# Two heads per penalty product, the penalty's bound on ScalarE, and other PSUM banks in the 16-head attention of the last layer

## The chip, the cores and the metric

The kernel runs on one core of a Trainium2 chip. A core has five engines that work side by side[...]: PE (TensorE, matrix products into the accumulator memory PSUM), VectorE (DVE in the profile), ScalarE (ACT), GpSimd (POOL) and SyncE (SP, which here issues most of the DMA transfers). Each engine takes its instructions in the order of the program. The metric is the device time of one execution in microseconds (us).

## The reference, cut to what matters

The network has four layers on an input of 16 x 256 x 128 numbers. Each layer normalizes, computes an attention and a feed-forward branch from the same normalized input, and adds their gated product to the residual. The change concerns the attention of the last layer, with 16 heads of width 8:

```python
g = sigmoid(hidden_states @ Wg + bg)                 # one number per token
Z_I, Z_J = g, swapaxes(g, 1, 2)
res = (1 - Z_I) * maximum(1 - Z_I - Z_J, 0) + Z_I * minimum(1 - Z_I + Z_J, 1)
scope = clip(power(s - 2, 1 - g) + 2 - abs_ij, 1e-32, 1)
log_pen = log(maximum(res * scope, 1e-32))           # 256 x 256 per batch element
scores = q @ k.T / sqrt(8) + log_pen                 # the same for all 16 heads
ctx = softmax(scores) @ v
```

The kernel does not add the logarithm. It multiplies the exponentials of the plain scores by the penalty itself, which is bounded from below by 1e-32.

## The kernel before, in words

**Where it stands.** `attn8` is called twice: by the first layer without a penalty, and by `attn3` for the last layer with one. The second call is the last stage of the kernel; after it only the last output remains to be stored. All earlier work of the last layer (its feed-forward branch in `xn`, the gates in `gates3`) is complete by then.

**Tiles.** There are 256 heads in all (16 batch elements, called batches here, of 16 heads). One head's scores are 256 x 256, held as 128 partitions x 512 numbers, which is one PSUM bank. Queries and keys are laid out so that a head occupies 8 of a group of 32 partitions, with a ninth row for the maximum.

**The loop.** The loop over `n` (line 446) works on two heads in each step. `scores(n, m)` (line 313) issues four matrix products that alternate: the first scores `pa` of head `n` (L322), queries by keys, and the second scores `pb` of head `m = n - 14` (L332), keys by queries, in which the maximum found from the first scores takes part. VectorE reduces `pa` to the negated row maximum `nmax` (L343). ScalarE takes the exponential of `pb` into `e` (L348). The tile `pb` then is free, and `e` waits for its product with the penalty.

**The product with the penalty.** `weaken(m)` (L311) multiplies `e` in place by the penalty tile `pens[m // 16]` of its batch. It is issued one step after the exponential, on VectorE for heads 2, 5, 9, 12 and 15 of each batch and on GpSimd for the other eleven.

**Around the heads.** Every eighth step (u is the step within eight, k within sixteen) other pieces are issued: at u = 1 `shifted` (L359, L365) transposes the maxima of the last eight heads and adds them to the queries, and `values` makes the value tile; at u = 3 `turn` (L400 to L408) transposes and divides the result of eight heads; at u = 5 `weigh` (L374) multiplies eight heads' `e` by the values, and ScalarE copies the result (L385). `project` (L272 to L288) makes queries and keys for two batches, sends them through memory and reads them back on SP's queue. `done` (line 1589) multiplies a finished batch by the feed-forward branch (L1594), adds it to the residual (L1595), and two steps later stores it from SP (L1592).

**The penalty.** `penalty(b)` in `attn3` (line 1511) returns a list of small functions that together make the penalty of a batch. The loop takes them one by one (line 479): ScalarE makes the four parts (L1532 to L1541), GpSimd the distance term `near` (L1544), two products `inner` (L1547, L1548) and their sum `summed` (L1551), and VectorE at k = 15 the product with the scope (L1554) and the lower bound (L1555). They are one batch ahead: batch b + 1's penalty is finished at step 15 of batch b and first used some 16 steps later.

**Buffers.** The first scores have three PSUM banks (`psa`), the second scores three (`psb`), all other products two (`psm`). There are 22 tiles `e`. A product into `pa` waits for the reduction three heads before, a product into `pb` for the exponential three heads before.

**What sets the order.** `pin(mark)` (line 484) chains each engine's instructions in the order in which the program issued them, so no planner reorders this stage: an instruction that waits holds back everything behind it on its engine.

Of the kernel before, what the change touches and what calls it, by code (L numbers as in the profile page):

```python
# [10 lines left out]
F32 = mybir.dt.float32  # L11
# [8 lines left out]
P = 128  # L20
B = 16
S = 256
# [51 lines left out]
class Net:  # L74
# [137 lines left out]
    def attn8(self, w, bias=None, wout=None, penalty=None, done=None):  # L212
# [16 lines left out]
        with ExitStack() as ctx:  # L229
            cp = ctx.enter_context(tc.tile_pool(name="at_c", bufs=1))  # L230
            pool = ctx.enter_context(tc.tile_pool(name="at", bufs=2))
            small = ctx.enter_context(tc.tile_pool(name="at_s", bufs=2))
            ep = ctx.enter_context(tc.tile_pool(name="at_e", bufs=22))
            dram = ctx.enter_context(tc.tile_pool(name="at_d", bufs=2, space=DRAM))
            psa = ctx.enter_context(tc.tile_pool(name="at_pa", bufs=3, space=PSUM))
            psb = ctx.enter_context(tc.tile_pool(name="at_pb", bufs=3, space=PSUM))
            psm = ctx.enter_context(tc.tile_pool(name="at_pm", bufs=2, space=PSUM))

            wqk = [self.load(cp, w[n], "w" + n) for n in "qk"]
# [64 lines left out]
                            va[:, q, :, 0:8], src, vadd.rearrange("p (h e) -> p h e", e=8)  # L304
                        )

            qas, es, pens, pos, zs = {}, {}, {}, {}, {}

            def weaken(m):
                eng = nc.vector if m % 16 in (2, 5, 9, 12, 15) else nc.gpsimd  # L310
                eng.tensor_mul(es[m], es[m], pens[m // 16])  # L311

            def scores(n, m):

                pa = psa.tile([P, 2, S], F32, name="pa") if n is not None else None
                pb = psb.tile([P, 2, S], F32, name="pb") if m is not None else None
                for t in range(2):
                    ts = slice(t * P, (t + 1) * P)
                    if n is not None:
                        b, h = divmod(n, 16)  # L320
                        r, g = 32 * (h % 4), h // 4
                        nc.tensor.matmul(  # L322
                            pa[:, t, :],
                            qbuf[b % 4][r : r + 32, g, ts],
                            kbuf[b % 4][r : r + 32, g, :],
                            start=True,
                            stop=True,
                        )
                    if m is not None:
                        b, h = divmod(m, 16)  # L330
                        r, g = 32 * (h % 4), h // 4
                        nc.tensor.matmul(  # L332
                            pb[:, t, :],
                            kbuf[b % 4][r : r + 32, g, ts],
                            qas[m // 8][r : r + 32, g % 2, :],
                            start=True,
                            stop=True,
                        )
                if penalty is not None and m is not None and m > 0:
                    weaken(m - 1)  # L340
                if n is not None:
                    u = n % 8
                    nc.vector.tensor_reduce(  # L343
                        nbuf[n // 8 % 2][:, :, u // 4, u % 4, 8], pa, AX.X, ALU.max, negate=True
                    )
                if m is not None:
                    e = ep.tile([P, 2, S], F32, name="e")
                    nc.scalar.activation(e, pb, AF.Exp, scale=scale)  # L348
                    es[m] = e
                    if penalty is not None and m == H - 1:  # L350
                        weaken(m)

            def shifted(i):

# [91 lines left out]
            for n in range(H + 4 * 8):  # L446
# [27 lines left out]
                if penalty is not None:  # L474
                    k = n % 16
                    if k == 0 and b + 2 < B:
                        parts[b + 2] = penalty(b + 2)
                        parts[b + 2].pop(0)()
                    if k in (3, 4, 5, 6, 7, 8, 9, 11, 13) and b + 1 < B:
                        parts[b + 1].pop(0)()  # L480
                    elif k == 15 and b + 1 < B:
                        pens[b + 1] = parts.pop(b + 1).pop(0)()
# [1016 lines left out]
    def attn3(self, g, dr, done):  # L1499
# [3 lines left out]
        with ExitStack() as ctx:  # L1503
# [2 lines left out]
            pool2 = ctx.enter_context(tc.tile_pool(name="a3_2", bufs=2))  # L1506
            pool3 = ctx.enter_context(tc.tile_pool(name="a3_3", bufs=3))
            dist = self.const("dist", cp, view="p (k q) -> p k q", k=2)
            wide = lambda t: t.rearrange("p (o q) -> p o q", o=1).to_broadcast([P, 2, S])

            def penalty(b):
# [31 lines left out]
                def near():  # L1543
                    nc.gpsimd.tensor_sub(sc, wide(pw), dist)  # L1544

                def inner():
                    nc.gpsimd.tensor_mul(lo, lo, wide(u))  # L1547
                    nc.gpsimd.tensor_mul(hi, hi, wide(gi))  # L1548

                def summed():  # L1550
                    nc.gpsimd.tensor_add(lo, lo, hi)  # L1551

                def bounded():
                    nc.vector.scalar_tensor_tensor(pen, sc, 1.0, lo, ALU.min, ALU.mult)  # L1554
                    nc.vector.tensor_scalar_max(pen, pen, 1e-32)  # L1555
                    return pen

                return [fetch, rest, low(0), low(1), high(0), high(1), rather, near, inner, summed, bounded]

            self.attn8(  # L1560
                {n: a["L3_attn_W" + n] for n in "qkv"},
# [6 lines left out]
    def layer3(self, out):  # L1568
# [5 lines left out]
        with ExitStack() as ctx:  # L1574
# [14 lines left out]
            def done(b, store):  # L1589
                ts = slice(2 * b, 2 * b + 2)  # L1590
                if store:
                    nc.sync.dma_start(out[:, ts, :], self.x[:, ts, :])  # L1592
                else:
                    nc.vector.tensor_mul(self.s[:, ts, :], self.s[:, ts, :], X[:, ts, :])  # L1594
                    nc.vector.tensor_add(self.x[:, ts, :], self.x[:, ts, :], self.s[:, ts, :])  # L1595

            self.attn3(g, dr, done)

# [375 lines left out]
```

## Time and profile before

| | |
|---|---|
| median of 3 runs | 3046.34 us (3040.31 to 3046.86) |
| profiled execution | 3046.38 us |
| its span, first to last instruction | 3044.6 us |
| mean TensorE clock granted | 0.879 |
| busy, share of the span: PE, VectorE, ScalarE, GpSimd | 83%, 69%, 49%, 44% |
| first product of the last stage (L322) | about 2612 us |
| last product of first scores (L322) | 3019.9 us |
| VectorE, ScalarE, GpSimd busy in 2820 to 2846 us | 22.92, 12.77, 20.86 us of 26 |

The profile is one execution. A row of groups gives line, engine, operation, written and read tiles with shapes and a count, then the busy time, the mean duration, the idle time of the engine just before, and what ended that idle time. Where two engines exclude each other, the time that an instruction stands inside the exclusion is part of its duration, so a long duration may be a wait. The clock column is the share of full speed that TensorE was granted. PE counts as busy from start to end of overlapping products, so a busy PE can still be slow.

### The profile page before, as it was taken

Reading aid. Unit: us, or ns where it says so; the run is one execution under the profiler, and the core shown is the slowest. Engines: PE = TensorE matmul, PEld = TensorE weight load, DVE = VectorE, ACT = ScalarE, POOL = GpSimd, SP = SyncE. Lnnn points to the kernel's source line nnn. Section 1 sums busy time; section 2 is a strip of 40 time slices with the busy share of each in tenths; the row PEclk is TensorE's granted clock in tenths of the full one; section 3 lists DMA queues with packets and bytes.
Section 4 is the critical chain, followed back from the end, with each engine's and each line's share of the span. In section 5 each row is a group of like instructions: output and inputs, shape, how many; then the busy total and the mean of one; then the engine's idle time right before and its main releaser. Section 6 shows DMA issues by size and latency. Waiting matters only on the chain.

```text
span 3044.6 us, 49166 instructions
## 1 busy us (share of the span) xinstructions
PE 2516.5 (83%) x17715; PEld 1627.3 (53%) x17743; DVE 2088.2 (69%) x4302; ACT 1506.0 (49%) x3339; POOL 1348.7 (44%) x1247
## 2 busy tenths in 40 slices
PE   5999882679665799999834899988799989798998
PEld 3666571556431466666513466665466655555555
DVE  4666433335487789888874778844687855588887
ACT  1555461223333566666531577751477764454554
POOL 2000002123227566656665455531455552487777
PEclk8999995879876899999965899998899999788888
DMA  2111002000113566666521000000100000211110
GB/s 64 29 29 29 6 3 99 1 16 15 40 57 123 153 178 184 182 175 185 170 72 49 15 13 15 13 5 1 44 14 14 15 10 1 49 37 38 31 39 10
DMA packets 155196, 168.95 MB, mean 55 GB/s; under 512 B 22817, under 2 KB 102874, under 8 KB 154954
## 3 DMA queue, kind: packets, MB, share of 16 engines
q1 hardware_dynamic: 146378, 147.71, 17.7%
q0 software_dynamic: 6496, 17.05, 1.7%
q8 instruction: 141, 2.31, 0.3%
q10 hardware_dynamic: 2080, 1.05, 0.1%
q14 instruction: 101, 0.83, 0.1%
HBM read 127.57 MB, written 29.79 MB: 52 GB/s over the span
## 4 chain that ended last, share of the span: by engine, by line
PE 29%; DVE 27%; ACT 7%; POOL 3%; issue 3%; DMA 2%; SPq 1%; another core or an unknown queue 0%; DVEq 0%; ACTq 0%; POOLq 0%
PE py L1145 4%; ACT p L1787 3%; PE pa L322 3%; DVE st L1124 2%; DVE nmax L343 2%; DVE rot L1713 2%; DVE ss L1712 2%; DVE sn L1716 2%; PE ph L1365 2%; PE py L1391 2%; DVE nm L1778 2%; PE ps L1768 2%; PE ph L1908 2%; PE pa L1000 1%; PE ph L1912 1%
## 5 line engine op out<-in xcount | busy, mean ns | idle before, releaser
L322 PE MATMUL pa<-kT,qT 32*128 32x256 f32 x2048 | 420.3, 443 | 54.6 <-DVE nmax L343 35.6
L343 DVE TENSOR_REDUCE nmax<-pa 128x2 f32<-128x512 f32 x512 | 332.1, 684 | 149.0 <-PE pb L332 123.4
L348 ACT ACTIVATE e<-pb 128x512 f32<-128x512 f32 x512 | 286.0, 595 | 295.4 <-PE pb L332 293.2
L332 PE MATMUL pb<-qa,kT 32*128 32x256 f32 x2048 | 414.6, 429 | 0.9 <-ACT e L348 0.9
L322 PEld LDWEIGHTS pa<-kT,qT 32*128 32x128 f32 x2048 | 273.9, 206 | 171.5 <-DVE nmax L343 80.8
L1135 POOL TENSOR_TENSOR hc<-st,cn 128x512 f32<-128x512 f32 x207 | 264.3, 1278 | 207.9 <-DVE dbb L1121 85.8
L1145 PE MATMUL py<-hc,ident 128*128 128x512 f32 x512 | 296.1, 670 | 68.6 <-DVE hc L1135 41.8
L1124 DVE TENSOR_TENSOR_SCAN st<-dab,dbb 128x512 f32<-128x512 f32 x256 | 312.5, 1221 | 33.0 <-ACT dab L1114 3.4
L311 POOL TENSOR_TENSOR e<-e,pen 128x512 f32<-128x512 f32 x176 | 241.7, 1390 | 102.4 <-ACT e L348 102.1
L332 PEld LDWEIGHTS pb<-qa,kT 32*128 32x128 f32 x2048 | 268.0, 199 | 7.9 <-ACT e L348 2.6
L1114 ACT ACTIVATE dab<-dl,A_log 128x512 f32<-128x512 f32 x256 | 181.5, 719 | 147.4 <-DVE st L1124 107.8
L1787 ACT ACTIVATE p<-ps,nm,rl 128x128 f32<-128x128 f32 x512 | 227.8, 466 | 30.0 <-DVE nm L1780 29.2
L1796 POOL TENSOR_TENSOR p<-p,den 128x512 f32<-128x512 f32 x128 | 133.0, 1040 | 231.5 <-DVE den L1795 225.9
L158 POOL TENSOR_SCALAR ln_r<-ln_mv 128x4 f32<-128x4 f32 x32 | 7.4, 232 | 493.5 <-DVE ln_st L168 419.4
L1698 PE MATMUL pm<-wqkv,hT 128*128 128x512 f32 x384 | 208.8, 658 | 17.9 <-DVE hT L1692 8.0
L1721 POOL TENSOR_TENSOR rot<-rot,sn 128x512 f32<-128x512 f32 x128 | 162.5, 1270 | 108.7 <-DVE sn L1716 71.3
L1121 DVE TENSOR_TENSOR dbb<-du,bn 128x512 f32<-128x512 f32 x256 | 203.1, 793 | 6.0
L1145 PEld LDWEIGHTS py<-hc,ident 128*128 128x128 f32 x512 | 94.6, 208 | 170.7 <-DVE hc L1135 68.3
L1711 ACT ACTIVATE sq<-pm 128x512 f32<-128x512 f32 x128 | 75.0, 617 | 136.2 <-PE pm L1698 136.2
L1768 PE MATMUL ps<-kT,qT 64*64 64x128 f32 x2048 | 137.2, 290 | 0.0
L374 PE MATMUL pm<-e,vaug 128*32 128x256 f32 x2048 | 133.2, 403 | 0.0
L1768 PEld LDWEIGHTS ps<-kT,qT 64*64 64x64 f32 x2048 | 91.2, 138 | 72.9 <-issue 70.1
(372 smaller groups left out, 5638.4 us busy)
## 6 DMA issues: line engine op xcount, KB each, us to landing
bn<-dr SPq DMA_DIRECT2D x128, 256.0 KB
cn<-dr SPq DMA_DIRECT2D x128, 256.0 KB
w<-in_L_ffn_W_dram SPq DMA_DIRECT2D x94, 256.0 KB
qkd<-qk SPq DMA_DIRECT2D x32, 256.0 KB
v<-v SPq DMA_DIRECT2D x64, 128.0 KB
f_y<-y SPq DMA_DIRECT2D x47, 128.0 KB
f_x<-zero POOLq DMA_DIRECT2D x8, 704.0 KB
xr<-f_x SPq DMA_DIRECT2D x44, 128.0 KB
```

The lines of the kernel that those rows point to most:

```text
L311: eng.tensor_mul(es[m], es[m], pens[m // 16])
L322: nc.tensor.matmul(pa[:, t, :], qbuf[b % 4][r : r + 32, g, ts], kbuf[b % 4][r : r + 32, g, :], start=True, stop=True,)
L332: nc.tensor.matmul(pb[:, t, :], kbuf[b % 4][r : r + 32, g, ts], qas[m // 8][r : r + 32, g % 2, :], start=True, stop=True,)
L343: nc.vector.tensor_reduce(nbuf[n // 8 % 2][:, :, u // 4, u % 4, 8], pa, AX.X, ALU.max, negate=True)
L348: nc.scalar.activation(e, pb, AF.Exp, scale=scale)
L1121: mul = nc.vector.tensor_mul(db, d["du"][:, h, :], d["bn", n])
L1124: nc.vector.tensor_tensor_scan(d["st", r], d.pop(("da", r)), db, 0.0, ALU.mult, ALU.add)
L1135: ins = eng.tensor_mul(d["hc", r], d.pop(("st", r)), d["cn", r // 2])
L1145: nc.tensor.matmul(d["py", h], self.ident, d.pop(("hc", r)), start=(n == 0), stop=(n == N - 1))
L1698: nc.tensor.matmul(pj, hTs[b % 3][:, t * P : (t + 1) * P], d["qkv"][:, j * 512 : (j + 1) * 512], start=True, stop=True,)
L1768: nc.tensor.matmul(ps[i][64 * half : 64 * half + 64, c, w, :], qT[f, 2 * u + c, q0 : q0 + 64], kT[f, 2 * u + c, keys[half] : keys[half] + ...
L1787: nc.scalar.activation(p[:, c, w, :], ps[i][:, c, w, :], AF.Exp, scale=r[:, w, 0, h + 2 * c : h + 2 * c + 1], bias=nm[:, c, w : w + 1], ac ...
```

## The change

With a penalty, `attn8` has four banks for first scores and two for second ones, and 11 tiles `e` of twice the size in place of 22. Two neighbouring heads share one such tile; `weaken` is issued in every second step for a pair, with the penalty tile read twice through a repeating dimension, on VectorE for the pairs that begin at heads 2 and 8 of a batch and on GpSimd for the other six. The lower bound of the penalty leaves VectorE: ScalarE computes Relu(pen - 1e-32) + 1e-32 in two activations, `over` and `least_of`. The penalty's parts are taken at other steps: `near` at k = 8, the two products of `inner` at 9 and 10, `summed` at 11, the VectorE product `bounded` at 13, `over` at 14 and `least_of` at 15. In `done` the last sum goes from VectorE to GpSimd. The call without a penalty keeps its banks and tiles.

```diff
--- before.py
+++ after.py
@@ -230,10 +230,10 @@
             cp = ctx.enter_context(tc.tile_pool(name="at_c", bufs=1))
             pool = ctx.enter_context(tc.tile_pool(name="at", bufs=2))
             small = ctx.enter_context(tc.tile_pool(name="at_s", bufs=2))
-            ep = ctx.enter_context(tc.tile_pool(name="at_e", bufs=22))
+            ep = ctx.enter_context(tc.tile_pool(name="at_e", bufs=11 if penalty else 22))
             dram = ctx.enter_context(tc.tile_pool(name="at_d", bufs=2, space=DRAM))
-            psa = ctx.enter_context(tc.tile_pool(name="at_pa", bufs=3, space=PSUM))
-            psb = ctx.enter_context(tc.tile_pool(name="at_pb", bufs=3, space=PSUM))
+            psa = ctx.enter_context(tc.tile_pool(name="at_pa", bufs=4 if penalty else 3, space=PSUM))
+            psb = ctx.enter_context(tc.tile_pool(name="at_pb", bufs=2 if penalty else 3, space=PSUM))
             psm = ctx.enter_context(tc.tile_pool(name="at_pm", bufs=2, space=PSUM))
 
             wqk = [self.load(cp, w[n], "w" + n) for n in "qk"]
@@ -304,11 +304,14 @@
                             va[:, q, :, 0:8], src, vadd.rearrange("p (h e) -> p h e", e=8)
                         )
 
-            qas, es, pens, pos, zs = {}, {}, {}, {}, {}
+            qas, es, pairs, pens, pos, zs = {}, {}, {}, {}, {}, {}
 
             def weaken(m):
-                eng = nc.vector if m % 16 in (2, 5, 9, 12, 15) else nc.gpsimd
-                eng.tensor_mul(es[m], es[m], pens[m // 16])
+
+                eng = nc.vector if m % 16 in (2, 8) else nc.gpsimd
+                pen = pens[m // 16].rearrange("p (o k) q -> p o k q", o=1)
+                eng.tensor_mul(pairs[m], pairs[m], pen.to_broadcast([P, 2, 2, S]))
+                del pairs[m]
 
             def scores(n, m):
 
@@ -336,19 +339,24 @@
                             start=True,
                             stop=True,
                         )
-                if penalty is not None and m is not None and m > 0:
-                    weaken(m - 1)
+                if penalty is not None and m is not None and m > 0 and m % 2 == 0:
+                    weaken(m - 2)
                 if n is not None:
                     u = n % 8
                     nc.vector.tensor_reduce(
                         nbuf[n // 8 % 2][:, :, u // 4, u % 4, 8], pa, AX.X, ALU.max, negate=True
                     )
                 if m is not None:
-                    e = ep.tile([P, 2, S], F32, name="e")
+                    if penalty is None:
+                        e = ep.tile([P, 2, S], F32, name="e")
+                    else:
+                        if m % 2 == 0:
+                            pairs[m] = ep.tile([P, 2, 2, S], F32, name="e")
+                        e = pairs[m - m % 2][:, m % 2]
                     nc.scalar.activation(e, pb, AF.Exp, scale=scale)
                     es[m] = e
                     if penalty is not None and m == H - 1:
-                        weaken(m)
+                        weaken(m - 1)
 
             def shifted(i):
 
@@ -476,7 +484,7 @@
                     if k == 0 and b + 2 < B:
                         parts[b + 2] = penalty(b + 2)
                         parts[b + 2].pop(0)()
-                    if k in (3, 4, 5, 6, 7, 8, 9, 11, 13) and b + 1 < B:
+                    if k in (2, 3, 4, 5, 6, 7, 8, 9, 10, 11, 13, 14) and b + 1 < B:
                         parts[b + 1].pop(0)()
                     elif k == 15 and b + 1 < B:
                         pens[b + 1] = parts.pop(b + 1).pop(0)()
@@ -1506,6 +1514,9 @@
             pool2 = ctx.enter_context(tc.tile_pool(name="a3_2", bufs=2))
             pool3 = ctx.enter_context(tc.tile_pool(name="a3_3", bufs=3))
             dist = self.const("dist", cp, view="p (k q) -> p k q", k=2)
+            least = cp.tile([P, 2], F32, name="least")
+            nc.gpsimd.memset(least[:, 0:1], -1e-32)
+            nc.gpsimd.memset(least[:, 1:2], 1e-32)
             wide = lambda t: t.rearrange("p (o q) -> p o q", o=1).to_broadcast([P, 2, S])
 
             def penalty(b):
@@ -1543,19 +1554,27 @@
                 def near():
                     nc.gpsimd.tensor_sub(sc, wide(pw), dist)
 
-                def inner():
-                    nc.gpsimd.tensor_mul(lo, lo, wide(u))
-                    nc.gpsimd.tensor_mul(hi, hi, wide(gi))
+                def inner(t, by):
+                    return lambda: nc.gpsimd.tensor_mul(t, t, wide(by))
 
                 def summed():
                     nc.gpsimd.tensor_add(lo, lo, hi)
 
                 def bounded():
                     nc.vector.scalar_tensor_tensor(pen, sc, 1.0, lo, ALU.min, ALU.mult)
-                    nc.vector.tensor_scalar_max(pen, pen, 1e-32)
+
+
+                def over():
+                    nc.scalar.activation(pen, pen, AF.Relu, bias=least[:, 0:1])
+
+                def least_of():
+                    nc.scalar.activation(pen, pen, AF.Identity, bias=least[:, 1:2])
                     return pen
 
-                return [fetch, rest, low(0), low(1), high(0), high(1), rather, near, inner, summed, bounded]
+                return [
+                    fetch, rest, low(0), low(1), high(0), high(1), rather, near,
+                    inner(lo, u), inner(hi, gi), summed, bounded, over, least_of,
+                ]
 
             self.attn8(
                 {n: a["L3_attn_W" + n] for n in "qkv"},
@@ -1592,7 +1611,7 @@
                     nc.sync.dma_start(out[:, ts, :], self.x[:, ts, :])
                 else:
                     nc.vector.tensor_mul(self.s[:, ts, :], self.s[:, ts, :], X[:, ts, :])
-                    nc.vector.tensor_add(self.x[:, ts, :], self.x[:, ts, :], self.s[:, ts, :])
+                    nc.gpsimd.tensor_add(self.x[:, ts, :], self.x[:, ts, :], self.s[:, ts, :])
 
             self.attn3(g, dr, done)
```

## The prediction

> **What bounds the kernel now.** The diff reaches only the last stage, the second call of `attn8`. I read its stage windows first, then its groups, the order of time on VectorE, and one-microsecond windows around a stall. The first windows set one stretch of the first layer's call of `attn8` (no penalty) beside one of the last layer's. Columns: stretch, then busy us and instructions of PE, weight load, VectorE, ScalarE, GpSimd; the clock granted to TensorE; DMA.
>
> ```profile
> 226.00:252.00 26.00, 25.10 (x306) 16.68 (x302) 18.79 (x38) 13.64 (x26) 0.00 (x0) 1.00 0.05 14
> 2820.00:2846.00 26.00, 24.31 (x212) 14.68 (x204) 22.92 (x34) 12.77 (x24) 20.86 (x15) 0.83 0.16 36
> ```
>
> The same products go at 306 matmul records per 26 us there and at 212 here. The starts of L1554 give the pace: 2654.21 to 2997.91 us is 13 batches, 26.44 us each. In thirteen 26-us windows (2638 to 2976) the means are VectorE 22.46 busy, GpSimd 20.67, ScalarE 12.94, PE 213 records at clock 0.848. At the first call's 305 records per 26 us, PE needs 26.44 x 213/305 = 18.5 us per batch at full clock. The lost clock adds 0.152 x 26.44 = 4.0 us, and 3.9 us is left for stalls.
>
> Groups of the steady part (2630 to 3000 us); after the shapes: busy us, mean ns, idle before:
>
> ```profile
> L322 PE MATMUL pa<-kT,qT 32*128 32x256 f32 x905 | 214.1, 453 | 34.4 <-DVE nmax L343 34.1
> L311 POOL TENSOR_TENSOR e<-e,pen 128x512 f32<-128x512 f32 x156 | 213.6, 1386 | 94.3 <-ACT e L348 94.1
> L343 DVE TENSOR_REDUCE nmax<-pa 128x2 f32<-128x512 f32 x226 | 148.0, 681 | 42.5 <-PE pb L332 42.5
> L322 PEld LDWEIGHTS pa<-kT,qT 32*128 32x128 f32 x904 | 137.3, 212 | 101.0 <-DVE nmax L343 61.8 <-issue 20.4 <-DVE s L408 5.4
> L311 DVE TENSOR_TENSOR e<-e,pen 128x512 f32<-128x512 f32 x70 | 76.8, 1097 | 3.9 <-ACT e L348 3.9
> L1554 DVE SCALAR_TENSOR_TENSOR pen<-sc,lo 128x512 f32<-128x512 f32 x15 | 25.7, 1711 | 2.4 <-POOL lo L1551 2.4
> L1555 DVE TENSOR_SCALAR pen<-pen 128x512 f32<-128x512 f32 x15 | 20.6, 1374 | 0.5
> L1595 DVE TENSOR_TENSOR x<-x,s 128x256 f32<-128x256 f32 x13 | 17.8, 1373 | 0.4
> L1594 DVE TENSOR_TENSOR s<-s,xn 128x256 f32<-128x256 f32 x13 | 13.7, 1051 | 0.0
> ```
>
> PE's stalls end on VectorE's reduction of the first scores, L343. And VectorE's other instructions are long: the shortest of the same forms took 0.68 (L311), 0.69 (L1554) and 0.43 us (L1555, L1595). The excess per batch is 5 x 0.42 + 1.02 + 0.94 + 0.94 + 0.62 = 5.6 us. In order of time:
>
> ```profile
> 2886.82 1.05 DVE L1594 TENSOR_TENSOR s<-s,xn 128x256 f32<-128x256 f32 x1
> 2887.91 1.38 DVE L1595 TENSOR_TENSOR x<-x,s 128x256 f32<-128x256 f32 x1
> 2889.20 0.68 DVE L343 TENSOR_REDUCE nmax<-pa 128x2 f32<-128x512 f32 x1
> 2889.81 1.15 DVE L311 TENSOR_TENSOR e<-e,pen 128x512 f32<-128x512 f32 x1
> 2892.11 1.74 DVE L1554 SCALAR_TENSOR_TENSOR pen<-sc,lo 128x512 f32<-128x512 f32 x1
> 2893.89 1.37 DVE L1555 TENSOR_SCALAR pen<-pen 128x512 f32<-128x512 f32 x1
> ```
>
> From step 12 to 17 of a batch only one reduction passes in some 2 us, PE's three first-score banks run full, and its clock falls:
>
> ```profile
> 2894.00:2895.00 1.00, 0.40 (x4) 0.00 (x0) 1.00 (x1) 0.47 (x1) 1.00 (x2) 1.00 0.32 99
> 2895.00:2896.00 1.00, 0.09 (x2) 0.09 (x2) 1.00 (x3) 0.13 (x1) 1.00 (x1) 1.00 0.48 82
> 2897.00:2898.00 1.00, 1.00 (x6) 0.69 (x4) 1.00 (x2) 0.60 (x1) 1.00 (x1) 0.50 0.57 95
> ```
>
> PE idles 1.5 us in two, and then runs at half clock. This comes back in every batch, for 3 to 11 us.
>
> **What the Trainium skill says.** "SBUF — State Buffer", section "Who interferes with whom": a VectorE instruction with two SBUF inputs and a GpSimd instruction that reads SBUF exclude each other for the whole instruction. The trace agrees: 0.69 us for L1554 alone, 1.74 beside GpSimd. "TensorE: Matmul & The Clock Gate", section "HAM oscillation — how this bites in real kernels": idle PE halves its clock. The trace agrees on the half, but less idleness than the page's 3.4 us is enough here (1.5 us above). Its opening table: ScalarE, VectorE and GpSimd queues are strict FIFO, so one waiting instruction holds what follows.
>
> **The change, part by part** (per batch; "held" is a duration less the 0.04 to 0.09 us in which the next one overlaps it).
>
> 1. Products for two heads. No 128x1024 product with a penalty is in the trace, but GpSimd's 128x1024 L1070 took 2.35 us and VectorE's L1062 1.23; a repeated operand costs GpSimd nothing (L1548, 1.27). GpSimd: 11 x 1.23 = 13.5 becomes 6 x 2.31 = 13.9. VectorE, without waits: 5 x 0.60 = 3.0 becomes 2 x 1.14 = 2.3. The unknown, a slower repeated pattern, I bound from 0 to 10% (1.6 us) and take 0.
> 2. Bound: VectorE loses L1555, 0.36 of work and 0.94 of waiting. ScalarE gains two 128x512 activations, 0.52 held by L1541, so 12.9 becomes 14.0 of 26: hidden by its idle time (uncovered, 15 x 1.04 = 16 us), unless it waits. It can: `over` (step 14) stands behind `bounded` (step 13), and later exponentials stand behind it.
> 3. The sum L1595 goes to GpSimd: VectorE loses 0.36 and 0.94 of waiting; GpSimd gains 0.69 (its 128x256 L592 took 0.73). The output store on SP waits for it some 2 us longer; behind it in SP's queue stand the next project's transfers, not used for 13 steps. Nothing on the path (uncovered, 2 us in every second batch, 16 us).
> 4. Steps spread out: the same instructions; GpSimd still has difference, two products, sum and one pair ahead of `bounded`.
> 5. Banks 4 + 2: PE may lead the reductions by four heads, the exponentials by two.
>
> VectorE's work falls from 22.46 - 5.6 = 16.8 to 15.4 us. Contended instructions fall from nine to four (two pairs, L1594, L1554), but each may meet a GpSimd instruction of 2.31 instead of 1.23. I bound the four waits by 0 and 9.2 us and take 4.4: 0.7 on each of three and 2.3 on L1554, which comes to its turn as the next pair starts. VectorE: 19.8, 2.6 less.
>
> The shared port is the new floor. GpSimd 13.9 + 4 x 1.23 + 0.69 = 19.5, VectorE's holds 2.3 + 0.61 + 0.36 = 3.2: together 22.7 us (before: 18.5 + 4.7 = 23.1).
>
> PE: 18.5 + 4.0 of lost clock + stalls. Step 13 stays the bad place. GpSimd needs, from step 8, about 1.2 (rest of a pair) + 1.2 + 1.2 + 1.1 (VectorE's pair) + 2.3 + 1.2 + 1.2 = 9.4 us until the sum is there, VectorE arrives after some 7, then the pair of heads 12 and 13 takes the port for 2.3 and L1554 needs 0.6: VectorE stands for 5.3 us. PE covers 2.1 (weighing) + 4 x 0.64 = 4.7, but the turn of the maxima at step 17 wants the reduction of step 15, 1.2 us later. The stall is 5.3 + 1.2 - 4.7 = 1.8 us where the port is that full, less after a slow-clock phase, in which GpSimd gets ahead. So PE: 18.5 + 4.0 + 1.8 = 24.3 us, above the floor, 2.1 less than now. Only 15 of the 16 batches have both halves of the loop: 15 x 2.1 = 32 us. In the drain GpSimd works without a gap (eleven L311 in 15.9 us from 3021.02); six pairs, two VectorE holds and a sum are 13.9 + 2.3 + 0.7 = 16.9, so about 1.5 us lost with the last sum on GpSimd. Net 30 us off the profiled execution's 3046.38 (span 3044.6, 1.8 outside), which agrees with the median 3046.34: **3016 us**. Its own range is 3000 to 3032 (stalls from 0.8 to 2.8 us).
>
> **Rivals.**
> - *Warm all the way (0.10).* Four banks cover the stall and PE keeps its clock: the port decides, 22.7 to 23.0 us, 15 x 3.5 - 1.5 = 51 us: 2995. For it: the first interval of L1554 (2630.83 to 2654.21), with PE warm, was 23.4 us. Against: a full port makes GpSimd late, so `bounded` waits.
> - *The stall only moves (0.13).* L1554 and its ScalarE followers hold PE as long as the three removed instructions did; still 26.4: 3042 to 3052, about 3048 with the drain. For it: PE now stalls 3.9 us, and a VectorE stop of 5.3 us is left.
> - *Slower (0.15).* `over` holds ScalarE behind `bounded`. With two second-score banks PE stops at step 17 until the exponential of step 15 has run. If the sum is one pair (2.3 us) later than above, the stall is 1.8 + 2.3, + 0.5 + 0.5 for `over` and that exponential: 5.1, against today's 3.9. 15 x 1.2 + 1.5 = 20 us: 3066. It decides once the stop passes 3.9 us per batch. Against: the products' inputs are early, and slow-clock phases let GpSimd catch up (it idles 5.7 us per batch now).
>
> **How the numbers follow.** Likeliest case 0.62. Under 0.2% (6 us) this kernel's measurement can't tell from no change. Of the second rival I count 0.04 faster, 0.05 same, 0.04 slower. Faster 0.62 + 0.10 + 0.04 = 0.76, same 0.05, slower 0.19. The range 2990 to 3052 takes in the first two rivals, with the 10% slower pattern (15 x 1.6 = 24 us on the likeliest, 3040), and leaves the slow one out.
>
> **What would show it.** Right: L1554 still long but its interval near 24.3 us; two pairs on VectorE of 1.2 to 3.5 us; PE's idle time before L322 well under 95 us; clock near 0.85 or above. Wrong: an interval of 26 us or more, PE waiting for L348, ScalarE waiting for L1554 by several us per batch, GpSimd pairs above 2.6 us uncontended, or weighing (L374) waiting for products.

## The result, and the profile after

| | before | after |
|---|---|---|
| median of 4 runs | 3046.60 us (3040.31 to 3054.01) | 3005.31 us (3002.19 to 3015.23) |
| profiled execution, span | 3046.38, 3044.6 us | 3015.23, 3013.5 us |
| first to last product of first scores (the loop) | 2611.6 to 3019.9, 408.3 us | 2611.5 to 2976.7, 365.2 us |
| from there to the end of the span (the drain) | 24.7 us | 36.8 us |
| one batch, 13 starts of the closing product apart | 26.44 us | 23.66 us |

The changed kernel takes 0.9869 of the time before, with a 95% interval of 0.9837 to 0.9901: some 41 us less. The two profiled executions differ by 31 us; that of the changed kernel was the slowest of its four (the others took 3002 to 3005 us). They reach the last stage at the same time; the loop is 43.1 us shorter and the drain 12.1 us longer. 13 x (26.44 - 23.66) = 36.1 us of the loop's gain lie in the steady batches. The "closing product" is VectorE's product of penalty and scope, L1554 before and L1564 after.

First the windows of the changed kernel: one in which the clock held, and the one that was shown of the kernel before (columns as there: busy us and instructions of PE, weight load, VectorE, ScalarE, GpSimd; clock; DMA).

```profile
2768.00:2794.00 26.00, 22.02 (x232) 14.14 (x230) 23.13 (x32) 16.75 (x32) 24.29 (x14) 1.00 0.25 57
...
2820.00:2846.00 26.00, 23.94 (x216) 14.65 (x214) 20.07 (x29) 14.11 (x27) 21.76 (x12) 0.83 0.28 55
```

Both kinds of stretch occur. Over eleven windows of 26 us (2660 to 2946) the mean clock is 0.915 against 0.846 before, and PE passes 240.6 records against 214.9. VectorE is busy 21.33 us of 26 (22.50 before), ScalarE 15.63 (13.02), GpSimd 23.18 (20.41): GpSimd now is the busiest engine after PE.

The groups of the steady part (2630 to 2970 us); after the shapes: busy us, mean ns, idle before.

```profile
L313 POOL TENSOR_TENSOR e<-e,pen 128x1024 f32<-128x1024 f32 x87 | 207.8, 2399 | 53.2 <-ACT e L356 52.5 <-DMA qT<-qkd 0.6
L335 PE MATMUL pb<-qa,kT 32*128 32x256 f32 x935 | 191.9, 435 | 24.3 <-ACT e L356 24.3
L325 PE MATMUL pa<-kT,qT 32*128 32x256 f32 x934 | 171.7, 437 | 0.0
...
L335 PEld LDWEIGHTS pb<-qa,kT 32*128 32x128 f32 x932 | 122.8, 202 | 46.6 <-ACT e L356 42.1
...
L313 DVE TENSOR_TENSOR e<-e,pen 128x1024 f32<-128x1024 f32 x30 | 56.9, 1898 | 3.8 <-ACT e L356 3.8
L1564 DVE SCALAR_TENSOR_TENSOR pen<-sc,lo 128x512 f32<-128x512 f32 x14 | 37.7, 2696 | 8.4 <-POOL lo L1561 8.4
...
L1568 ACT ACTIVATE pen<-pen,least 128x512 f32<-128x512 f32 x14 | 10.1, 722 | 17.2 <-DVE pen L1564 17.2
```

PE's waits have changed sides. Before, its products and weight loads of first scores waited 34.1 and 61.8 us for VectorE's reductions; now the products of first scores don't wait for them at all and their weight loads for 5.5 us, and the second scores wait 24.3 and 42.1 us for the exponentials: PE runs into the two banks for second scores. The closing product is longer than it was (2.70 against 1.71 us), since it now stands behind a pair of heads. The order on VectorE in one batch (start, duration):

```profile
2836.07 0.56 DVE L1613 TENSOR_TENSOR s<-s,xn 128x256 f32<-128x256 f32 x1
...
2837.81 2.82 DVE L1564 SCALAR_TENSOR_TENSOR pen<-sc,lo 128x512 f32<-128x512 f32 x1 [0.57 <-POOL lo L1561]
2840.55 1.87 DVE L346 TENSOR_REDUCE nmax<-pa 128x2 f32<-128x512 f32 x3
```

VectorE waits 0.57 us for GpSimd's sum, then stands 2.82 us, and three reductions follow without a product between. One-microsecond windows show what PE does meanwhile:

```profile
2839.00:2840.00 1.00, 0.65 (x8) 0.51 (x7) 1.00 (x1) 0.41 (x1) 1.00 (x1) 1.00 0.00 0
2840.00:2841.00 1.00, 0.59 (x6) 0.18 (x1) 1.00 (x2) 0.34 (x1) 1.00 (x2) 1.00 0.08 16
2841.00:2842.00 1.00, 0.08 (x2) 0.08 (x2) 1.00 (x3) 1.00 (x3) 1.00 (x2) 1.00 0.00 0
...
2843.00:2844.00 1.00, 1.00 (x5) 0.69 (x4) 0.36 (x1) 0.60 (x1) 1.00 (x2) 0.50 0.36 84
```

So a stall is still there in this place: PE idles 1.7 of 3 us (0.35 + 0.41 + 0.92) and then runs at half clock. It now ends on the exponentials, not on the reductions: PE waits 1.3 us for an exponential until 2841.92, and that stood behind `over`, which waited for the closing product. Single batches now lie between 22.1 and 25.5 us apart: 22.1 to 23.2 in the seven with a mean clock of 0.92 or more (23.15 in each of the three with 1.00), 23.9 to 25.5 in the six with 0.86 or 0.87. Before, they were 25.8 to 27.5, and 25.8 to 25.9 in those with a clock of 0.92.

### The profile page after: what moved, and what is told of

It is laid out like the page before. It is cut to its first block, busy times and chain, and to the rows that moved or that the text cites. A ratio compares the mean times of both kernels' runs of the same rounds, so it can differ in the third digit from the quotient of the medians.

```text
span 3013.5 us, 48937 instructions
## 1 busy us (share of the span) xinstructions
PE 2490.4 (83%) x17715; PEld 1618.9 (54%) x17743; DVE 2033.4 (67%) x4222; ACT 1523.9 (51%) x3371; POOL 1352.7 (45%) x1185
## 3 DMA queue, kind: packets, MB, share of 16 engines
q8 instruction: 141, 2.31, 0.3%
## 4 chain that ended last, share of the span: by engine, by line
PE 27%; DVE 23%; POOL 8%; ACT 8%; issue 4%; DMA 2%; SPq 1%; another core or an unknown queue 0%; DVEq 0%; POOLq 0%; ACTq 0%
PE py L1153 5%; ACT p L1806 3%; POOL e L313 3%; DVE st L1132 2%; DVE rot L1732 2%; DVE ss L1731 2%; DVE sn L1735 2%; PE py L1399 2%; PE ph L1373 2%; DVE nm L1797 2%; PE ps L1787 2%; PE ph L1927 2%; PE pa L1008 1%; PE pa L325 1%; PE ph L1931 1%
## 5 line engine op out<-in xcount | busy, mean ns | idle before, releaser
L335 PE MATMUL pb<-qa,kT 32*128 32x256 f32 x2048 | 387.3, 422 | 26.5 <-ACT e L356 26.5
L356 ACT ACTIVATE e<-pb 128x512 f32<-128x512 f32 x512 | 286.2, 594 | 228.4 <-PE pb L335 207.2
L325 PE MATMUL pa<-kT,qT 32*128 32x256 f32 x2048 | 367.1, 435 | 19.2 <-DMA kT<-qkd 17.7
L1132 DVE TENSOR_TENSOR_SCAN st<-dab,dbb 128x512 f32<-128x512 f32 x256 | 312.5, 1221 | 34.1 <-ACT dab L1122 4.5
L325 PEld LDWEIGHTS pa<-kT,qT 32*128 32x128 f32 x2048 | 232.7, 200 | 103.3 <-issue 55.4
L335 PEld LDWEIGHTS pb<-qa,kT 32*128 32x128 f32 x2048 | 249.7, 195 | 55.4 <-ACT e L356 47.0
L313 POOL TENSOR_TENSOR e<-e,pen 128x1024 f32<-128x1024 f32 x96 | 228.9, 2395 | 59.1 <-ACT e L356 58.3
```

What stands on the lines that cost most here:

```text
L313: eng.tensor_mul(pairs[m], pairs[m], pen.to_broadcast([P, 2, 2, S]))
L325: nc.tensor.matmul(pa[:, t, :], qbuf[b % 4][r : r + 32, g, ts], kbuf[b % 4][r : r + 32, g, :], start=True, stop=True,)
L335: nc.tensor.matmul(pb[:, t, :], kbuf[b % 4][r : r + 32, g, ts], qas[m // 8][r : r + 32, g % 2, :], start=True, stop=True,)
L1132: nc.vector.tensor_tensor_scan(d["st", r], d.pop(("da", r)), db, 0.0, ALU.mult, ALU.add)
```

## The experiments

The kernel before moved between medians of 3034 and 3047 us from one set of runs to the next, so the ratio to the runs beside each kernel is compared, not its time (the three sets below ran on three different chips). Loop and drain are those of one profiled execution each. The theories named in the expectations are these. **Port**: each instruction that no longer competes with GpSimd for the shared access to SBUF is worth its work and its wait; so each of the three offloads (pairs, bound, sum) should cost its share when undone. **Banks**: four banks of first scores cover the stall. **Steps**: the gain comes from the closing product, two steps earlier. **Offload**: it comes from the bound and the sum leaving VectorE.

### One part undone in the changed kernel

Banks (`u_banks`):

```diff
-            psa = ctx.enter_context(tc.tile_pool(name="at_pa", bufs=4 if penalty else 3, space=PSUM))
-            psb = ctx.enter_context(tc.tile_pool(name="at_pb", bufs=2 if penalty else 3, space=PSUM))
+            psa = ctx.enter_context(tc.tile_pool(name="at_pa", bufs=3, space=PSUM))
+            psb = ctx.enter_context(tc.tile_pool(name="at_pb", bufs=3, space=PSUM))
```

> The changed kernel with three banks for first scores and three for second ones again; all else as changed. Port theory (the gain is VectorE's: four instructions that contend for the port in place of nine): within 10 us of 3005, the interval of the penalty product (L1564) 23 to 24.5 us, PE's waiting for the exponentials (some 65 us in the changed kernel) under 30 us and its waiting for the reductions up in its place. Banks theory (the gain is PE's lead of four heads): 3030 to 3047, most of the 41 us gone.

Pairs (`u_pairs`), with `ep` at 22 tiles, one tile for each head and `weaken(m - 1)` in every step:

```diff
-                eng = nc.vector if m % 16 in (2, 8) else nc.gpsimd
-                pen = pens[m // 16].rearrange("p (o k) q -> p o k q", o=1)
-                eng.tensor_mul(pairs[m], pairs[m], pen.to_broadcast([P, 2, 2, S]))
-                del pairs[m]
+                eng = nc.vector if m % 16 in (2, 5, 9, 12, 15) else nc.gpsimd
+                eng.tensor_mul(es[m], es[m], pens[m // 16])
```

> The changed kernel with one product per head again (five of sixteen on VectorE, 22 tiles); all else as changed. Port theory: VectorE gets back 0.7 us of work and three more contended instructions per batch, each with a shorter wait; together 1 to 2 us per batch, 3020 to 3035, less if the shorter waits pay for the number. Rival (pairs only hurt, since a wait for a GpSimd pair is twice as long): 2990 to 3004, faster than the changed kernel.

Bound (`u_bound`), at step 14; `least_of` only returns the tile:

```diff
                 def over():
-                    nc.scalar.activation(pen, pen, AF.Relu, bias=least[:, 0:1])
+                    nc.vector.tensor_scalar_max(pen, pen, 1e-32)
 
                 def least_of():
-                    nc.scalar.activation(pen, pen, AF.Identity, bias=least[:, 1:2])
                     return pen
```

> The changed kernel with the lower bound on VectorE again, as one instruction at step 14; all else as changed. Port theory: 0.36 us of work and a wait of up to 2.3 us behind a GpSimd pair, right after the long L1564: 1.5 to 2.5 us per batch, 3025 to 3045. Rival (ScalarE's two activations behind L1564 hold PE through the two second-score banks and cost as much): 2995 to 3010.

Sum (`u_sum`):

```diff
-                    nc.gpsimd.tensor_add(self.x[:, ts, :], self.x[:, ts, :], self.s[:, ts, :])
+                    nc.vector.tensor_add(self.x[:, ts, :], self.x[:, ts, :], self.s[:, ts, :])
```

> The changed kernel with the last sum on VectorE again; all else as changed. Port theory: 0.36 us of work and a wait of 1 to 2.3 us per batch ahead of L1564, which waits for GpSimd anyway, so part of it is covered: 3010 to 3030; the end after the last sum shorter by 1 to 3.5 us. Rival (covered whole by L1564's wait): 3000 to 3008.

Measured in one set (kernel before 3037.38 us beside them):

| kernel | median us | ratio to before (95%) | loop, us | drain, us |
|---|---|---|---|---|
| all parts | 3005.31 | 0.9869 (0.9837 to 0.9901) | 365.2 | 36.8 |
| banks undone | 2996.68 | 0.9866 (0.9842 to 0.9890) | 365.7 | 30.0 |
| pairs undone | 3006.14 | 0.9894 (0.9870 to 0.9919) | 359.8 | 37.2 |
| bound undone | 3001.05 | 0.9872 (0.9849 to 0.9895) | 360.3 | 37.3 |
| sum undone | 3000.69 | 0.9871 (0.9846 to 0.9895) | 360.9 | 37.7 |

The row of all parts is the result above, from another set. None of the four undone parts costs anything that these intervals, some 0.25% to either side, can tell from zero. Banks undone came out as the port theory had it: within 10 us of 3005, the closing products 23.4 us apart, and PE's waiting back on the reductions. Pairs undone lies between the two ranges that were given. The port theory's additive prices for the bound and the sum miss: the part comes back and the time does not, and both kernels lie in the range of their rival. What the parts' instructions did is seen in the groups. Of the kernel with the bound back on VectorE (2660 to 2940 us, as all groups from here on):

```profile
L1568 DVE TENSOR_SCALAR pen<-pen 128x512 f32<-128x512 f32 x12 | 4.9, 411 | 0.0
```

At step 14 the bound takes 0.41 us (mean of 12), where the same instruction took 1.37 at step 15 of the kernel before: it waits for no GpSimd instruction there. PE's waits show that the rival's reason holds as well, that ScalarE's two activations cost PE about as much as the bound on VectorE does. A row of waits gives the waiting engine with tile and line, what it waited for, then the total in us, the count and the longest. The changed kernel:

```profile
PEld pb L335 <- ACT e L356: 32.5, 42, 2.0
```

and with the bound on VectorE:

```profile
PEld pm L367 <- DVE nmax L346: 16.5, 12, 2.7
PEld pb L335 <- ACT e L356: 13.0, 30, 0.8
```

PE's weight loads wait 19.5 us less for exponentials and 16.5 us more for a reduction, at the turn of the maxima (L367 in `shifted`), where the changed kernel shows no such wait. And of the kernel with the sum back on VectorE:

```profile
L1564 DVE SCALAR_TENSOR_TENSOR pen<-sc,lo 128x512 f32<-128x512 f32 x13 | 29.0, 2234 | 0.0
...
L1614 DVE TENSOR_TENSOR x<-x,s 128x256 f32<-128x256 f32 x13 | 18.0, 1387 | 0.4
```

The sum waits again (1.39 us), but the closing product behind it shrinks from 2.68 to 2.23 us and no longer waits for `lo` (0.43 us per batch in the changed kernel, 5.1 / 12 in the same window). So of the 1.39 us that the sum takes, VectorE would otherwise have spent 0.88 us before or in the closing product.

### Parts alone on the kernel before, and the changed kernel again

Banks alone (`o_banks`) and pairs alone (`o_pairs`) are the diff's own lines for these parts and nothing else.

> The kernel before with four banks for first scores and two for second ones with the penalty; all else as before. Port theory: 3035 to 3055, no clear difference. Banks theory: 3005 to 3025.

> The kernel before with one product for two heads (pairs 2 and 8 on VectorE, 11 double tiles); the bound, the last sum, the steps and the banks as before. Port theory: VectorE loses 0.7 us of work and three contended instructions, but the bound, the two closing products and L1554 each wait for up to 2.3 us instead of 1.2: 3035 to 3055. If pairs carry the gain by themselves: 3010 to 3025.

Everything but pairs and banks (`o_moved`): the bound on ScalarE, the sum on GpSimd and the new steps, with single heads and three banks each. Then the changed kernel once more (`again`), for comparison in the same set.

> The kernel before with the bound on ScalarE, the last sum on GpSimd and the new steps of the penalty's parts; one product per head and three and three banks as before. Port theory: VectorE loses 0.7 us of work and 1.9 us of waiting per batch, 15 x 2 = 30 us: 3010 to 3025. Banks theory or pairs theory: 3035 to 3050.

> The changed kernel once more beside the others of this call: 3000 to 3016. Its end after the last sum shows whether the 6.5 us there (3.1 before the change) come again: if they belong to the sum on GpSimd they do, within 0.5 us.

Measured (before: 3033.94 us):

| kernel | median us | ratio (95%) | loop, us | drain, us |
|---|---|---|---|---|
| banks alone | 3036.64 | 1.0001 (0.9987 to 1.0014) | 403.0 | 30.0 |
| pairs alone | 3050.28 | 1.0048 (1.0031 to 1.0065) | 420.0 | 29.9 |
| bound, sum and steps | 3003.35 | 0.9900 (0.9882 to 0.9919) | 375.2 | 28.8 |
| the changed kernel again | 3003.20 | 0.9882 (0.9861 to 0.9903) | 363.5 | 34.7 |

The banks theory falls: four banks alone change nothing in the total. They do move time from one end of the stage to the other. From the first product to the first steady closing product it is 39.9 us with them and 42.6 in the kernel before (36.6 in the changed kernel, 39.7 with its banks undone), and the drain is 5.3 us longer; the steady batches are 26.4 us with and without. Within the loop of the changed kernel they choose what PE waits for, exponentials with two banks for second scores, reductions with three, as here with the banks undone:

```profile
PEld pa L325 <- DVE nmax L346: 36.5, 49, 2.2
```

Pairs alone make the kernel slower. Their groups show where the time goes:

```profile
L1602 DVE TENSOR_TENSOR x<-x,s 128x256 f32<-128x256 f32 x11 | 27.1, 2463 | 0.4
L1562 DVE TENSOR_SCALAR pen<-pen 128x512 f32<-128x512 f32 x10 | 24.5, 2449 | 0.3
L1561 DVE SCALAR_TENSOR_TENSOR pen<-sc,lo 128x512 f32<-128x512 f32 x10 | 22.6, 2261 | 0.0
```

The same three instructions took 1.37, 1.37 and 1.71 us before. They now stand beside GpSimd products of 2.35 us where they were half as long: 2.7 us more per batch in the bad place, and a batch takes 27.4 us (26.4 before). Bound, sum and steps together give most of the whole gain without the other two parts. Their 30 us are what the port theory's sum of prices gave (15 x 2 us), but the next two runs show that the prices are not the reason. The changed kernel came again as expected, also in its end (6.4 us).

### Steps and offload apart

Steps alone (`o_steps`): the new list of steps and the divided `inner`, with bound and sum left on VectorE (`bounded` at 13, the bound at 14).

```diff
-                    if k in (3, 4, 5, 6, 7, 8, 9, 11, 13) and b + 1 < B:
+                    if k in (2, 3, 4, 5, 6, 7, 8, 9, 10, 11, 13, 14) and b + 1 < B:
...
                     nc.vector.scalar_tensor_tensor(pen, sc, 1.0, lo, ALU.min, ALU.mult)
+
+                def over():
                     nc.vector.tensor_scalar_max(pen, pen, 1e-32)
```

> The kernel before with the new steps of the penalty's parts alone: the closing product at step 13, the bound on VectorE at step 14, the products of two parts at 9 and 10, their sum at 11; the last sum on VectorE, one product per head, three and three banks. Steps theory (where VectorE's contended instructions stand decides, and no longer how many there are): from the first to the last product of first scores 365 to 380 us (408 before, 365 with the whole change), 3000 to 3015 in all. Offload theory (the bound or the sum must leave VectorE; either one is enough): 395 to 408 us, 3028 to 3040 beside a kernel before of 3034 to 3046. Both parts needed: between these.

Offload alone (`o_offload`): the old steps; the two activations follow the closing product at step 15, and the sum is on GpSimd.

```diff
                     nc.vector.scalar_tensor_tensor(pen, sc, 1.0, lo, ALU.min, ALU.mult)
-                    nc.vector.tensor_scalar_max(pen, pen, 1e-32)
+                    nc.scalar.activation(pen, pen, AF.Relu, bias=least[:, 0:1])
+                    nc.scalar.activation(pen, pen, AF.Identity, bias=least[:, 1:2])
...
-                    nc.vector.tensor_add(self.x[:, ts, :], self.x[:, ts, :], self.s[:, ts, :])
+                    nc.gpsimd.tensor_add(self.x[:, ts, :], self.x[:, ts, :], self.s[:, ts, :])
```

> The kernel before with the bound on ScalarE and the last sum on GpSimd alone, at the steps of before (both activations at step 15 behind the closing product); one product per head, three and three banks. Offload theory: from the first to the last product of first scores 365 to 380 us, 3000 to 3015 in all. Steps theory: 395 to 408 us, 3028 to 3040. Both parts needed: between these.

Measured (before: 3045.47 us): steps alone 3036.11 us, ratio 0.9969 (0.9958 to 0.9981); offload alone 3057.20 us, ratio 1.0036 (1.0018 to 1.0054). The loops are 394.6 and 415.9 us. Neither theory stands: steps alone lies where the offload theory had put it (to 0.4 us), but offload alone is slower than any range that was given. The two effects alone come to -0.31% + 0.36%, about nothing; together (`o_moved`, another set) they are -1.0%. This is an interaction. The waits of offload alone show the one half of it:

```profile
ACT pen L1558 <- DVE pen L1557: 49.2, 10, 5.3
...
DVE pen L1557 <- POOL lo L1554: 18.6, 10, 1.9
...
DVE e L311 <- ACT e L348: 17.2, 21, 1.4
```

VectorE, relieved (19.11 us busy of 26), comes early to the closing product and waits 1.9 us for GpSimd's sum. ScalarE, which now has to bound the product at once, stands 4.9 us per batch in front of it, with the exponentials behind. These then keep VectorE waiting in turn: its own products with the penalty wait 17.2 us for exponentials (2.9 in the kernel before), and the reductions stand behind them. With the new steps ScalarE's wait is 2.2 us per batch (bound, sum and steps):

```profile
ACT pen L1561 <- DVE pen L1557: 25.8, 12, 2.2
```

Steps alone show the other half. The closing product and the bound meet less of GpSimd, but VectorE stays full:

```profile
L1553 DVE SCALAR_TENSOR_TENSOR pen<-sc,lo 128x512 f32<-128x512 f32 x11 | 12.6, 1148 | 0.0
L1556 DVE TENSOR_SCALAR pen<-pen 128x512 f32<-128x512 f32 x12 | 10.6, 881 | 0.0
```

VectorE is still busy 22.45 us of 26, the clock is 0.83 in all eleven windows, and a batch takes 25.6 us. With the offload added (`o_moved`) it takes 24.1, with the offload alone 27.0 (each from 13 starts of the closing product). The new list moves the closing product two steps ahead and also puts one step between it and its follow-up; no run separates the two.

### The end, and three pairs on VectorE

`end_vector`: the changed kernel with 3 + 3 banks (as above) and the last batch's sum on VectorE. `three_pairs`: the same with a third pair on VectorE.

```diff
-                    nc.gpsimd.tensor_add(self.x[:, ts, :], self.x[:, ts, :], self.s[:, ts, :])
+                    eng = nc.vector if b == B - 1 else nc.gpsimd
+                    eng.tensor_add(self.x[:, ts, :], self.x[:, ts, :], self.s[:, ts, :])
```

> The changed kernel with three and three banks and the last sum of the last batch alone on VectorE. If the 6.5 us between the last store's issue and the end (3.1 us where that sum is VectorE's) belong to the sum on GpSimd, the end comes 3.4 us sooner than with the three and three banks alone: 2990 to 2998. If they belong to something else: 2993 to 3002, and 6.5 us at the end.

```diff
-                eng = nc.vector if m % 16 in (2, 8) else nc.gpsimd
+                eng = nc.vector if m % 16 in (2, 8, 12) else nc.gpsimd
```

> As end_vector, and the pair of heads 12 and 13 on VectorE, so that GpSimd has five pairs. A GpSimd pair holds the port for 2.31 us, a VectorE pair for 1.14, so the port's floor falls from 22.7 to 21.5 us per batch, and the closing product no longer waits for that pair. If the port sets the pace of batches at full clock: 1 us per batch, 2975 to 2988. If VectorE's time does (it is busy 21 to 22 us of 26): 2990 to 3010.

Measured (before: 3045.47 us): `end_vector` 3005.56 us, ratio 0.9873 (0.9855 to 0.9890); `three_pairs` 2992.84 us, ratio 0.9841 (0.9823 to 0.9859), the fastest of all. In the profiles the end from the last store's issue is 3.1 us in both, as the first theory had it. The total of `end_vector` does not show the 3.4 us and lies above both ranges: the kernel before was 8 us slower in this set than beside the banks undone, and the last stage starts anywhere between 2594 and 2620 us in the profiled executions, though the stages ahead of it have the same code in all these kernels.

`three_pairs` lies 5 us above the port theory's range (2975 to 2988) and in that of VectorE's time (2990 to 3010). The order on VectorE:

```profile
2824.18 2.08 DVE L313 TENSOR_TENSOR e<-e,pen 128x1024 f32<-128x1024 f32 x1
...
2826.79 0.41 DVE L1613 TENSOR_TENSOR s<-s,xn 128x256 f32<-128x256 f32 x1
...
2827.73 0.82 DVE L1564 SCALAR_TENSOR_TENSOR pen<-sc,lo 128x512 f32<-128x512 f32 x1
```

GpSimd's pair of heads 12 and 13 no longer takes the port just ahead of the closing product, GpSimd waits for VectorE's L1613 instead (25.5 us in 13 batches), and the closing product takes 0.82 us in place of 2.24 to 2.82. This part of the expectation is met. The pace of the port is not: in `end_vector`, which differs by this pair alone, the batches at clock 1.00 are 22.6 us apart (one is 23.2), and in `three_pairs` 22.2 to 22.3, so they gain 0.3 us where the computed floor falls by 1.2. The larger gain is the clock. In `end_vector` every second batch from 2797 us on takes 25.2 us at a clock of 0.86; in `three_pairs` the clock is 1.00 in all eleven windows, and from 2672 us on every batch has the short time. Its loop is 353.9 us, that of `end_vector` 368.0.

## Why the prediction was right or wrong, point by point

**The total.** 3016 us was predicted for the profiled execution and it took 3015.23. To 1 us this is luck. The loop was to gain 31.5 us and gained 43.1; the drain was to lose 1.5 and lost 12.1. The median, 3005, is nearer to what the runs repeat, and lies within the likeliest case's own range of 3000 to 3032.

**PE's sum per batch, 18.5 + 4.0 + 1.8 = 24.3 us.** It measured 23.66. The mis-sized terms are two, in opposite directions. "4.0 of lost clock" was carried over from the kernel before; it is 0.085 x 23.66 = 2.0 us. The stalls, 1.8, are what remains: 23.66 - 18.5 - 2.0 = 3.2 us. So the gain is 2.1 us of clock and 0.7 us of stalls, where I had put it all on stalls. A stall and the clock that it costs belong together; holding one fixed while shortening the other was the error. How much clock a stall costs can't be read from the idle time alone: in the three batches at 1.00 PE idled 2.8 to 2.9 us, in gaps spread over the batch. What decides it stays open. The remaining 7 us of the loop's gain lie at its two ends: 6.0 before the first steady batch (42.6 us from the first product to that closing product before, 36.6 after) and 0.9 behind the last. Some 3 of the 6.0 go with the four banks, which I had not priced there: the changed kernel with 3 + 3 banks takes 39.7 us. The first run of products of first scores (40 records before, 38 after) takes 10.63 against 8.39 us, both at a clock of 0.50, and as long as before with the banks undone.

**Where PE stalls.** I had PE covered by four banks until the turn of the maxima asks for the reduction of step 15. In the changed kernel no such wait shows; PE stops at the two banks for second scores. "PE waiting for L348" (L356 now) was on my own list of signs of being wrong, and it came: 24.3 and 42.1 us. So the size of the stall was near and its path was not. The path that I described is the one of the kernel with the bound on VectorE (16.5 us at L367, above).

**The shared port as the floor, 22.7 us.** The size is right: batches at clock 1.00 take 23.15 us in the changed kernel, 22.6 to 23.2 with its banks undone, 22.5 with its sum undone. A floor it is not for a single batch: with the bound undone such batches take 21.9 us, each beside a longer one. Nor is it shown to set the pace: a third pair on VectorE lowers the computed floor to 22.7 - 2.31 + 1.14 = 21.5 us, and the batches at full clock fell from 22.6 to 22.27 only. The rivals "warm all the way" and "the stall only moves" each describe some of the batches; neither holds throughout.

**Parts 1 to 4.** The sizes are right. VectorE was to be busy 19.8 us per batch and is 21.33 x 23.66 / 26 = 19.4. (My 22.46 was for 26 us; for a batch of 26.44 it is 22.8, and the sum then 20.2.) ScalarE was to need 14.0 us of 26.44 and needs 15.63 x 23.66 / 26 = 14.2. GpSimd's pair takes 2.34 us at the least, as L1070 does without a repeated operand, so a repeated penalty costs nothing. The wait of 2.3 us in L1564 is 2.82 - 0.69 = 2.1. What I had not seen is that part 4, which I had entered as "the same instructions", gives the gain only together with parts 2 and 3, and they only with it, at least in the kernel before: my sum gives each offload its own price, and the runs with one part undone or one part alone show that these prices do not add. In the kernel before, parts 2 and 3 alone cost 0.36%, and part 1 alone 0.48%.

**Where ScalarE stands.** The "slower" rival rested on `over` holding ScalarE. It does so for 1.2 us per batch (17.2 / 14), and PE's stalls, 3.2 us by the sum above, stayed under the 3.9 us at which I had put the turning point. Offload alone, at the old steps and with single heads and three banks each, comes near that rival, with ScalarE held for 4.9 us per batch and a kernel 0.36% slower. There PE's stalls still end on the reductions for the most part (products and weight loads together wait 65.0 us in 280 for these and 17.2 for exponentials), so the hold seems to act through VectorE's queue and not through the banks for second scores.

**Banks (part 5).** I gave them no price, but my estimate of the stall used their cover (4 x 0.64 us). The runs with and without them can't be told apart. What they gain came at the start of the stage (above), and their price in the drain, which I had not worked out for PE at all. In windows of 5 us from the last product of first scores on, the changed kernel:

```profile
2986.70:2991.70 5.00, 4.08 (x16) 2.73 (x16) 1.23 (x1) 2.50 (x5) 2.31 (x2) 0.80 0.00 2
2991.70:2996.70 5.00, 5.00 (x33) 2.90 (x36) 2.25 (x3) 1.68 (x3) 4.19 (x4) 0.50 0.00 0
2996.70:3001.70 5.00, 4.24 (x38) 1.89 (x32) 0.55 (x2) 0.59 (x1) 1.69 (x1) 0.50 0.12 30
```

and the same kernel with 3 + 3 banks:

```profile
2968.10:2973.10 5.00, 4.34 (x55) 2.62 (x53) 1.15 (x4) 3.02 (x7) 4.79 (x2) 1.00 0.01 2
2973.10:2978.10 5.00, 4.99 (x55) 3.04 (x53) 2.90 (x4) 3.01 (x6) 3.81 (x3) 1.00 0.02 3
```

With two banks PE is busy 13.0 of the first 15 us and then drops to half clock, and the drain lasts 36.8 us; with three it is busy 14.3 and stays at 1.00, and the drain lasts 30.0. All five profiles of the changed order with 4 + 2 banks have 34.7 to 37.7 us, the four with 3 + 3 banks 26.4 to 30.6. Two banks are not the only way to it: `three_pairs` and steps alone dip to 0.50 in the drain too, with 30.6 and 30.8 us. By these profiles 6.8 of the 12.1 us (36.8 - 30.0) go with the banks, 3.4 are the end (below), and 1.9 are left for the GpSimd work that I had priced at 1.5; but two profiles of the changed kernel itself differ by 2.1 us (36.8, 34.7), so the last figure shows nothing.

**"The sum: nothing on the path".** Wrong at the very end. The last lines of the changed kernel's timeline (span 3013.5 us):

```profile
3006.28 0.72 POOL L1614 TENSOR_TENSOR x<-x,s 128x256 f32<-128x256 f32 x1 [7.89 <-DVE s L1613]
3007.03 0.37 SPq L1611 DMA_DIRECT2D out_dram<-x  x1
```

From the store's issue to the end it is 6.5 us, against 3.1 in the kernel before.

**What stays open.** The smallest set of parts that gives the gain. The steps and at least one of bound and sum are needed when pairs and banks are absent, or both are: steps with the sum only, or the bound only, were not tried there, nor pairs and banks with the steps but without offload. Nor is it settled how long a gap costs PE its clock, or what limits `three_pairs` at 22.27 us, above its computed floor. That VectorE's shorter stand is what keeps the clock up is read from the order of events in the traces; no run changed the stalls alone.

## What to carry to other kernels

Where two engines exclude each other, price a stretch by the order of instructions on its slowest engine, not by adding up what each removed instruction costs: the next one in the queue can take the wait over. Before a follow-up goes to another in-order engine, see that its producer is done by then; the same offload lost 0.4% behind a late producer and was part of a gain of 1.0% behind an early one. And work out the drain by itself: a choice of buffers that changes nothing in the steady batches can gain some microseconds while the stage fills and lose more while it drains.

## What the hardware showed beyond that

- In these kernels the end of the program depends on the engine that made the last stored tile. From the last store's issue to the end of the span it is 6.4 to 6.5 us in the seven kernels that had the last sum on GpSimd, and 3.1 to 3.2 us in the seven with it on VectorE. The transfer itself landed within 2 us in the kernel before and in the changed one. What passes in the other 3.4 us no trace shows.
- A wait for the shared access grew with the other engine's instruction: VectorE's bound and sum took 1.37 us beside GpSimd products of one head and 2.45 us beside pairs. "SBUF — State Buffer", "Who interferes with whom", in the Trainium skill says that the lock is held for a whole instruction, and this agrees. The bound took 0.41 us at a step where it met none.
